# Macaron block on one core: attention scores in units of 32 queries for all heads, and half of the query blocks taken straight from the bank of the maxima

## The chip, the cores and the metric

The kernel runs on one core of one Trainium2 chip. The metric is device time in microseconds (us) of one launch, the median of a few runs.

## The reference

The input is x, 16 batches of 512 positions of 128 features, all in float32. Three residual steps follow each other: half a feed-forward step, an attention step, half a feed-forward step, each on the layer-normalised input.

```python
x = x + 0.5 * ffn(layernorm(x))      # ffn: x @ int4-rounded kernel + bias + (x @ a) @ b
x = x + attn(layernorm(x))           # 16 heads, causal
x = x + 0.5 * ffn(layernorm(x))
# attn: q = x Wq (16 heads of 64); latent = x Wkv_down (32 wide, shared by all heads)
#       k = latent Wk_up, v = latent Wv_up
#       y = softmax(mask(q k^T / 8)) v; result = y Wout
```

## The kernel before

**The algebra.** Query and key weights are multiplied once at the start, and so are value and output weights. Each head then has a 32-wide query against one 32-wide latent per key, and that latent is also the value. The 16 heads stand as 4 groups (`g`) of 4 heads (`h`); the four heads of a group lie on the four blocks of 32 partitions. `qt` holds the queries, `kt` the latents with features on partitions (the same four times), `lat` the latents with keys on partitions.

**Two passes over the scores.** The softmax needs the maximum of each query's scores, and the outputs need the probabilities with keys on partitions. So each score is computed twice. The S pass (`s_parts`, banks `sx`) puts queries on partitions and keys along the free axis; TensorE adds the causal mask of the last 128 by 128 block with small bfloat16 products (`mask_w`), and VectorE takes the negated maxima (`find_maxima`, L651 and L655). GpSimd splits the maxima into three bfloat16 terms (`maxima`, L728 to L732), and TensorE turns them into rows (`maxima_t`, tile `rows`). The T pass (`t_parts`, banks `tx`) puts keys on partitions and queries along the free axis; TensorE adds the turned maxima with bfloat16 products against `ones_u`, ScalarE takes the exponential (`exponentials`, L664, tile `pt`), and GpSimd zeroes the probabilities above the diagonal (`zeros`, L677).

**Outputs and sums.** `values` multiplies `lat` with `pt` for a group's four heads side by side, 128 by 32 products into the bank `o` (L763). The softmax's sums come from products with ones; GpSimd first adds blocks of `pt` so that fewer products are needed (`add_01`, `add_2`, `add_23`, lines L747, L752, L757). The sums go through DRAM to a compact form, VectorE takes reciprocals, DRAM broadcasts them (`rb`), and GpSimd multiplies (`normalise`, L839). `tail` projects with the merged value and output weights (`yp`), adds the residual, and does the second feed-forward step.

**The order.** It is written out by hand, under a manual schedule. A step is one `burst`: an S unit of 512 keys' worth of columns for four heads, and beside it a T unit of the same size of six steps earlier (`LAG`). `STEP` lists the five kinds of unit of a pair of groups; a batch has ten steps, 160 steps in all. `merge` interleaves the two streams so that heads 0 and 1 of T run beside heads 2 and 3 of S on the four row blocks of the array, and then the other way round. A burst has two S tiles of two banks each (pool `ps_s`, two buffers, 4 banks), and four T banks (pool `ps_t`, four buffers). Everything else is put between bursts: `plan` gives the pieces of `front` (layer norms, first feed-forward step, keys, queries), `latent`, `normalised` (the layer norms' inverse roots, with three VectorE operations in `ln_newton`, L344 to L346) and `tail` due times in steps. The last units, with no S work left, have bursts of their own (`late_burst`, `late_outputs`, `divided`, `last_tail`).

Of the kernel before, what the change touches and what calls it, by code (L numbers as in the profile page):

```python
# [25 lines left out]
def macaron_kernel(  # L26
# [24 lines left out]
    assert D == P and NT * P == L and L <= 512 and HG == 4 and H % HG == 0  # L51
    scale = HD**-0.5
# [4 lines left out]
    io = ctx.enter_context(tc.tile_pool(name="io", bufs=3))  # L57
# [54 lines left out]
    def load_heads(src, n, name):  # L112
        t = const.tile([P, NW, n], F32, tag=name, name=name)
        nc.sync.dma_start(t, src.rearrange("(t p) n -> p t n", p=P))
        return t

    wq_sb = load_heads(wq_t, D, "wq_sb")
    wk_sb = load_heads(wk_t, LD, "wk_sb")
    xs[1] = load_x(1)
    zs[1] = load_blocks(x[1], "a1")  # L120
    wv_sb = load_heads(wv_t, LD, "wv_sb")
    wo_sb = load_heads(wout, D, "wo_sb")
# [8 lines left out]
    terms = []  # L131
    for k in range(2):
        t3 = const.tile([P, NT, P], BF16, tag=f"terms{k}", name=f"terms{k}")
        nc.vector.memset(t3, 0.0)
        terms.append(t3)
    ones_u = const.tile([P, 2, P], BF16, tag="ones_u", name="ones_u")
# [6 lines left out]
    eye_b = const.tile([P, LD], BF16, tag="eye_b", name="eye_b")  # L143
    for h in range(HG):
        rows = slice(h * LD, (h + 1) * LD)
        nc.vector.tensor_copy(eye_b[rows, :], ident[rows, ts(h, LD)])
    eye2_b = const.tile([P, 2, LD], BF16, tag="eye2_b", name="eye2_b")
    for k in range(2):
        nc.vector.tensor_copy(eye2_b[:, k, :], eye_b)
    for u in range(2):  # L150
        pick = const.tile([P, 1], F32, tag=f"pick{u}", name=f"pick{u}")
        nc.vector.tensor_reduce(pick, ident.rearrange("p (h c) -> p c h", c=LD)[:, 3 * u : 3 * u + 3, :], AX.XY, ALU.max)
        nc.vector.tensor_scalar(ones_u[:, u, :], ones_f, pick, None, ALU.mult)


    mask_w = const.tile([P, NT, P], BF16, tag="mask_w", name="mask_w")
    nc.gpsimd.memset(mask_w, 0.0)

    def masks():
        for h in range(HG):  # L160
            rows = slice(h * LD, (h + 1) * LD)
            nc.gpsimd.affine_select(
                mask_w[rows, :, :], mask_w[rows, :, :], pattern=[[-LD, NT], [1, P]],
                compare_op=ALU.is_ge, fill=MASK, base=0, channel_multiplier=-1,
            )
# [87 lines left out]
    wqk_raw = act2.tile([P, L], F32, tag="osb", name="wqk_raw", bufs=4)[:, : NW * 2 * LD].rearrange(  # L253
# [97 lines left out]
    def ln_scale(src, name, ln):  # L351

        xn = act2.tile([P, NT, D], F32, tag="xn", name=f"xn_{name}")
        for t in range(NT):
            nc.scalar.activation(xn[:, t, :], src[:, t, :], AF.Copy, scale=rstd(ln, "b", t))  # L355
        return xn
# [7 lines left out]
    def turn_blocks(z, name, tag):  # L364
        xt = act2.tile([P, L], F32, tag=tag, name=f"{tag}_{name}")
# [3 lines left out]
    def turn(src, name, tag):  # L369
# [3 lines left out]
        xt = act2.tile([P, L], F32, tag=tag, name=f"{tag}_{name}")  # L373
# [3 lines left out]
    def with_bias(src, name, engine):  # L377
        xb = act2.tile([P, NT, D], F32, tag="xb", name=f"xb_{name}")
# [10 lines left out]
    def ffn(xt, ln, xb, name, tag, bufs):  # L389


        return ffn_out(ffn_product(xt, name), ln, xb, name, tag, bufs)

# [6 lines left out]
    def ffn_out(fp, ln, xb, name, tag, bufs):  # L400
        dst = io.tile([P, NT, D], F32, tag=tag, name=f"{tag}_{name}", bufs=bufs)
# [16 lines left out]
    def normalised(w):  # L418
        whats = [k for k, b in (("c", w - 2), ("b", w + 2), ("a", w + 3)) if 0 <= b < (B - 2 if k == "c" else B)]
# [7 lines left out]
    def front(b, st):  # L427
# [23 lines left out]
        x1 = st["x1"] = ffn(xt, la, xb, na, "x1", 5)  # L451
# [11 lines left out]
        xnt = turn_blocks(z, nb, "xnt_b") if b else turn(xn, nb, "xnt_b")  # L463
        yield
        mp = take(f"kt_ps_{b}")
        kt = st["kt"] = act2.tile([P, L], F32, tag="kt", name=f"kt_{b}", bufs=3)
# [21 lines left out]
        def query(g):  # L488
            mp = take(f"qt_ps_{b}_{g}")
            product(mp, wqk_flat[:, ts(g, P)], xnt)  # L490
            if g % 2 == 0:
                st["qt", g] = act2.tile([P, 2, L], F32, tag="qt", name=f"qt_{b}_{g}", bufs=4)
            nc.scalar.copy(st["qt", g - g % 2][:, g % 2, :], mp)  # L493

        yield
        query(0)
        yield
        query(1)
        yield
        query(2)  # L500
        yield
        query(3)
        yield

    def latent(b, st):

        lat = st["lat"] = act2.tile([P, NT, LD], F32, tag="lat", name=f"lat_{b}", bufs=3)
        for m in range(HG):
            keys = st["kt"][ts(m, LD), :].rearrange("c (t m r) -> c t m r", t=NT, m=HG)
            nc.vector.transpose(lat[ts(m, LD), :, :], keys[:, :, m, :])  # L510
        yield
# [3 lines left out]
    FRONT_STEPS = (-31, -30.5, -29, -28, -21, -19.25, -16, -16, -13, -10.5, -8, -4.25, -4, -3.5, -3.25, -2, 3, 4)  # L515
    SECOND_STEPS = (-9.5, -8.5, -7, -5.5, -5, -4.25, -4, -3.5, -3.25, -2, 3, 4)
    THIRD_STEPS = (-18.5, -18.5, -18.5, -18, -17.5, -17.25, -16, -16) + FRONT_STEPS[8:]
    FOURTH_STEPS = (-27, -26, -25.5, -25) + FRONT_STEPS[4:]
    TAIL_STEPS = (1.75, 2.5, 2.75, 3.5, 4.5, 7, 7, 7.75, 10.5)
    NORMALISED_STEPS = (5, 6)  # L520

    def tail(b, st, late=False):


# [38 lines left out]
        yield  # L563

# [544 lines left out]
```

## Time and profile before

| | |
|---|---|
| median of 3 runs | 810.46 us (810.18 to 812.5) |
| span of the profiled execution | 808.8 us, mean granted TensorE clock 0.995 |
| TensorE busy | 786.1 us, 97% |
| VectorE busy | 620.9 us, 77% |
| ScalarE busy | 488.1 us, 60% |
| GpSimd busy | 676.1 us, 84% |
| first S unit starts | 30.28 us into the span |
| first late burst starts | 767.76 us into the span |

The profile's span runs from the first to the last instruction of one execution; the median of the runs is 1.7 us longer. In the profile PE is TensorE's products, PEld its weight loads, DVE is VectorE, ACT is ScalarE, POOL is GpSimd and SP issues most transfers. A product in float32 stands as two instructions on TensorE, one for each of two passes. A line such as L651 is that of the instruction in the program; all products of a burst carry the line of `merge`, L641.

### The profile page before, as it was taken

How to read it: one execution, taken by the hardware profiler on the slowest of the kernel's cores; microseconds unless marked ns; L12 is line 12 of the kernel's file. 1: busy time of each engine (PE TensorE's matmuls, PEld its weight loads, DVE VectorE, ACT ScalarE, POOL GpSimd, SP SyncE). 2: the span in 40 equal slices, each digit the busy share in tenths (PEclk: the TensorE clock that was granted, in tenths of full speed). 3: DMA queues.
4: the chain of work that ended last, by engine and by line, in shares of the span. 5: the costliest groups of instructions: out<-in, count | busy, mean ns of one | idle time of the engine just before them, and what ended most of it. 6: DMA issues, size and time to landing. Idle time of an engine off the chain costs nothing.

```text
span 808.8 us, 35715 instructions
## 1 busy us (share of the span) xinstructions
PE 786.1 (97%) x15400; PEld 507.6 (63%) x15400; DVE 620.9 (77%) x1318; ACT 488.1 (60%) x971; POOL 676.1 (84%) x675
## 2 busy tenths in 40 slices
PE   7899999999999999999999999999999999999987
PEld 5556566675666667666666666666566666666644
DVE  7887886878878697877869787777978777686817
ACT  1237675657566675756657575666657666665661
POOL 1018989999988999989899898989989979998992
PEclk9989999999999999999999999999999999999999
DMA  5123122232422323332232423223223222211201
GB/s 138 28 57 68 32 69 68 65 72 73 95 61 70 80 62 83 74 83 60 70 89 55 93 63 82 69 61 93 51 53 77 58 63 66 70 44 47 58 24 48
DMA packets 171022, 54.01 MB, mean 67 GB/s; under 512 B 119512, under 2 KB 162680, under 8 KB 170864
## 3 DMA queue, kind: packets, MB, share of 16 engines
q1 hardware_dynamic: 170096, 51.44, 27.2%
q8 instruction: 120, 1.97, 1.0%
q10 hardware_dynamic: 768, 0.30, 0.1%
q14 instruction: 38, 0.31, 0.1%
HBM read 37.90 MB, written 13.80 MB: 64 GB/s over the span
## 4 chain that ended last, share of the span: by engine, by line
PE 70%; DVE 9%; POOL 6%; DMA 5%; ACT 5%; SPq 2%; issue 2%; DVEq 0%; POOLq 0%; ACTq 0%
PE sx L641 17%; PE o L763 14%; PE tx L641 13%; PE s L763 7%; PE qt_ps L385 6%; PE yp L385 6%; DVE nmax L651 3%; POOL b L747 3%; DMA rb<-recs 2%; PE fp_c L385 2%; ACT xn_b L355 2%; DMA recs<-rec 2%; PE fp_a L385 1%; POOL ot L839 1%; ACT pt L664 1%
## 5 line engine op out<-in xcount | busy, mean ns | idle before, releaser
L651 DVE TENSOR_REDUCE nmax<-sx 128x2 f32<-128x768 f32 (+2 forms) x384 | 312.6, 863 | 105.9 <-PE tx L641 67.6
L664 ACT ACTIVATE pt<-tx 128x512 f32<-128x512 f32 x616 | 319.5, 598 | 85.3 <-PE tx L641 78.8
L641 PE MATMUL sx<-kt,qt 32*128 32x512 f32 (+3 forms) x2048 | 324.4, 444 | 0.0
L641 PE MATMUL tx<-qt,kt 32*128 32x512 f32 x1728 | 319.3, 469 | 0.0
L747 POOL TENSOR_TENSOR b<-pt,pt 128x768 f32<-128x768 f32 x126 | 226.8, 1822 | 0.5
L641 PEld LDWEIGHTS sx<-kt,qt 32*128 32x128 f32 x2048 | 176.8, 186 | 24.7 <-issue 1.0
L677 POOL TENSOR_SCALAR_AFFINE_SELECT pt<-pt 128x1024 f32<-128x1024 f32 (+1 forms) x162 | 144.8, 900 | 17.2 <-ACT pt L664 15.4
L763 PE MATMUL o<-pt,lat 128*32 128x512 f32 x1984 | 146.4, 435 | 0.8 <-POOL pt L677 0.8
L641 PEld LDWEIGHTS tx<-qt,kt 32*128 32x128 f32 x1728 | 131.5, 185 | 5.1
L763 PEld LDWEIGHTS o<-pt,lat 128*32 128x32 f32 x1984 | 62.5, 109 | 77.9 <-issue 59.0
L641 PE MATMUL tx<-rows,ones_u 6*128 6x512 bf16 (+1 forms) x988 | 109.9, 297 | 1.1 <-DVE wvo L292 0.5
L839 POOL TENSOR_TENSOR ot<-osb,rb 128x512 f32<-128x512 f32 x62 | 79.0, 1275 | 35.9 <-DMA rb<-recs 33.6
L655 DVE TENSOR_REDUCE nmax<-sx 128x4 f32<-128x1024 f32 x64 | 75.4, 1219 | 31.9 <-PE tx L641 31.8
L782 ACT COPY osb<-o 128x512 f32<-128x512 f32 x62 | 36.3, 585 | 92.1 <-PE o L763 92.1
L641 PE MATMUL sx<-eye_b,mask_w 32*128 32x64 bf16 (+1 forms) x2560 | 87.8, 183 | 2.4 <-DVE nmax L655 1.7
L641 PEld LDWEIGHTS <-ones_u 6*128 6x128 bf16 x1024 | 43.1, 92 | 74.3 <-issue 61.6
L641 PEld LDWEIGHTS <-mask_w 32*128 32x128 bf16 x2560 | 67.4, 92 | 32.7 <-issue 24.6
L752 POOL TENSOR_TENSOR b<-b,pt 128x512 f32<-128x512 f32 x63 | 80.5, 1278 | 5.1
L757 POOL TENSOR_TENSOR b<-pt,pt 128x512 f32<-128x512 f32 x63 | 80.4, 1276 | 0.1
L385 PE MATMUL qt_ps<-xnt_b_b,wqk 128*32 128x512 f32 x512 | 68.0, 603 | 0.2
L763 PE MATMUL s<-b,ones_f 128*32 128x384 f32 x992 | 65.1, 380 | 3.1 <-POOL b L752 2.6
L493 ACT COPY qt<-qt_ps 128x512 f32<-128x512 f32 x64 | 37.5, 586 | 48.4 <-PE qt_ps L385 48.4
(194 smaller groups left out, 815.6 us busy)
## 6 DMA issues: line engine op xcount, KB each, us to landing
rb<-recs SPq DMA_DIRECT2D x248, 64.0 KB
x<-in_x_dram SPq DMA_DIRECT2D x16, 256.0 KB
sums<-ssb SPq DMA_DIRECT2D x248, 2.0 KB
z_a<-in_x_dram SPq DMA_DIRECT2D x60, 64.0 KB
blocks_b<-xn_b SPq DMA_DIRECT2D x15, 256.0 KB
z_b<-blocks_b SPq DMA_DIRECT2D x60, 64.0 KB
kt<-kt_d SPq DMA_DIRECT2D x60, 64.0 KB
out_dram<-x_c SPq DMA_DIRECT2D x15, 256.0 KB
```

Source lines behind the costliest of these rows:

```text
L385: nc.tensor.matmul(dst[ts(h, LD), :], lhsT=w[:, ts(h, LD)], rhs=mv, start=start, stop=stop, skip_group_check=True)
L493: nc.scalar.copy(st["qt", g - g % 2][:, g % 2, :], mp)
L641: nc.tensor.matmul(dst, lhsT=w, rhs=mv, start=first, stop=last, skip_group_check=True)
L651: nc.vector.tensor_reduce(nmax[:, i, heads, u], sx[:, :, col : col + (i + 1) * P], AX.X, ALU.max, negate=True)
L655: nc.vector.tensor_reduce(nmax[:, 1, heads, :], sx.rearrange("p k (u n) -> p k u n", u=2), AX.X, ALU.max, negate=True)
L664: nc.scalar.activation(pt[:, :, 2 * pair + k, :], tx[k].rearrange("p (b n) -> p b n", n=P), AF.Exp)
L677: nc.gpsimd.affine_select(diag, diag, pattern=[[0, diag.shape[1]], [1, P]], compare_op=ALU.is_ge, fill=0.0, base=0, channel_multiplier=-1,)
L747: nc.gpsimd.tensor_tensor(*flat, ALU.add)
L752: nc.gpsimd.tensor_tensor(b01, b01, st["pt", 2, g][:, u], ALU.add)
L757: nc.gpsimd.tensor_tensor(both, st["pt", 2, g][:, 2 + u], st["pt", 1, g + u][:, 0], ALU.add)
L763: nc.tensor.matmul(dst[ts(h, LD), :].rearrange("p (b n) -> p b n", n=P), lhsT=w[h] if isinstance(w, list) else w, rhs=mv, start=start, sto ...
L839: nc.gpsimd.tensor_tensor(turned(st)[:, g, :], st["osb", g], st["rb", g], ALU.mult)
```

## The change

A unit is no longer four heads of one group and 128 queries; it is all 16 heads and 32 queries. The queries are stored as query-major, group-minor (`qt` as 512 times 4), so that 128 columns are 32 queries by 4 groups, and the four row blocks carry the four `r` of a group. Each of the 16 query blocks of a batch has its own key width, a multiple of 32. Nine S units cover a batch (`S_UNITS`), seven T units cover its second 256 queries (`T_UNITS`).

- **Query blocks 0 to 7** (the first 256 queries, "short") have no T pass. ScalarE takes the exponential straight from the S bank with the maximum as bias, and keeps the sum along the row (`short_exponentials`). VectorE turns the result in 32 by 32 blocks in the next step (`turn_short`). Outputs are 128 products per batch of 32 by 32 weights (`short_values`), once all of a batch is turned. The sums need no products (`short_reciprocals`).
- **Query blocks 8 to 15** go as before, except that the causal mask of the T pass is now in the bfloat16 products (`diag_w`), so GpSimd's `zeros` is gone. GpSimd adds whole `pt` tiles (128 by 2048) five times a batch (`add`), and `sums` streams two added tiles instead of summing per group.
- S masks are four small products per unit (`tri`, `eye4`) instead of sixteen.
- The order is again written out by hand, nine steps a batch, 144 in all. The special ending is gone: the loop runs on until all planned work is done.

```diff
+    S_UNITS = ((12, 2), (13, 1), (14, 0), (15,), (7,), (8, 6), (9, 5), (10, 4), (11, 3))
+    T_UNITS = {5: (3, 0), 6: (3, 1), 7: (3, 2), 8: (3, 3), 10: (2, 0), 11: (2, 1), 12: (2, 2)}
+    SHORT = 2 * NT
...
     def find_maxima(...):
+        for qb, (w, col) in zip(unit, widths(unit)):
+            nc.vector.tensor_reduce(
+                st["nmax"][:, slot(qb), ts(pair, 2)], sx[:, :, col : col + w], AX.X, ALU.max, negate=True
+            )
+    def exponentials(tx, st, unit, pair):
...
+        for k in range(2):
+            nc.scalar.activation(pt[:, 2 * pair + k, :], tx[k], AF.Exp)
+    def short_exponentials(sx, st, unit, pair):
...
+        for qb, w, col in mine:
+            pq = probs.tile([P, 2, L // 2], F32, tag="pq", name=..., bufs=4)
+            for k in range(2):
+                r = 2 * pair + k
+                nc.scalar.activation(
+                    pq[:, k, :w], sx[:, k, col : col + w], AF.Exp, bias=st["nmax"][:, slot(qb), r : r + 1],
+                    accum_out=st["total"][:, qb // NT, r, qb % NT : qb % NT + 1],
+                )
+            turning.append((st, qb, pair, pq[:, :, :w]))
+    def turn_short():
+        while turning:
+            st, qb, pair, pq = turning.popleft()
+            nc.vector.transpose(
+                st["short"][:, ts(pair, 2), : qb + 1, qb, :], pq.rearrange("p k (n c) -> p k n c", c=LD)
+            )
     def burst(n, s_at, t_at, t_unit):
...
+        for k in range(2):
+            if s_at:
+                find_maxima(ss[k], s_at, s_unit, 1 - k)
+            if t_at:
+                exponentials(tt[k], t_at, t_unit, k)
+        for k in range(2):
+            if s_at:
+                short_exponentials(ss[k], s_at, s_unit, 1 - k)
-    def zeros(st, g, kind, u, heads=slice(0, 4)):
...
+    def add(st, name, one, two):
...
+        nc.gpsimd.tensor_tensor(st[name], st[one], st[two], ALU.add)
+    def values(st, i):
+        o_ps = take(f"o_{st['b']}_{i}")
+        for j in range(i + 1):
+            streamed(o_ps, st["lat"][:, j, :], st["pt", i, j], j == 0)
+        st["osb", i] = act2.tile([P, L], F32, tag="osb", name=..., bufs=3)
+        nc.scalar.copy(st["osb", i], o_ps)
+    def short_values(st):
+        banks = [take(f"o_{st['b']}_s{p}") for p in range(HG)]
+        for kb in range(SHORT):
+            for p in range(HG):
+                rows = ts(p, LD)
+                for r in range(HG):
+                    nc.tensor.matmul(
+                        banks[p][ts(r, LD), kb * LD : SHORT * LD], lhsT=st["lat32"][rows, kb, :],
+                        rhs=st["short"][rows, r, kb, kb:, :].rearrange("p n c -> p (n c)"), ...
+                    )
...
+        for p in range(HG):
+            nc.scalar.copy(...)          # 4 copies of 128 by 256, out of the four banks
+    def short_reciprocals(st):
+        nc.vector.reciprocal(rec, st["total"]...)   # 128 by 32
+        nc.vector.transpose(rec_t, rec)
...
+    GAPS = {
+        0: ((short_values, (), 1), (maxima_t, (2,), 1)),
+        4: ((values, (2,), 1), (maxima_t, (3,), 0)),
+        5: ((sums, (3,), 1),),
+        6: ((sums, (2,), 1),),
+        8: ((values, (3,), 0),),
+    }
+    NORMALISED = {5: ((0, 1), (1, 1)), 0: ((3, 2),), 1: ((2, 2),)}
+    ADDED = {
+        7: (("a3", ("pt", 3, 0), ("pt", 3, 1), 0),),
+        0: (("a3b", ("pt", 3, 2), ("pt", 3, 3), 1),),
+        1: (("a3", "a3", "a3b", 1),),
+        3: (("a2", ("pt", 2, 0), ("pt", 2, 1), 1),),
+        4: (("a2", "a2", ("pt", 2, 2), 1),),
+    }
+    TERMS = {3: slice(0, 4), 8: slice(4, 8)}
...
+    while n < END or todo:
+        turn_short()
+        parts(n - 0.5)
+        for name, one, two, lag in ADDED.get(s, ()): ...   # add
+        burst(n, batch(n, 0), *t_due(n))
...                                                        # maxima, normalise
+        parts(n - 0.25)
+        for what, which, lag in GAPS.get(s, ()): ...
+        parts(n)                                           # NORMALISED_STEPS = (5, 6): ln_newton at step 6
...
-    late_burst((st, gp), 4)
...
-    last_tail(st, yp, late_tail)
```

## The prediction

> **What bounds the kernel now.** I read the page first, then the windows of three batches in mid-run, then the groups kept apart by shape, then the timeline around single bursts and around the layer norm's small operations.
>
> ```profile
> PE 786.1 (97%) x15400; PEld 507.6 (63%) x15400; DVE 620.9 (77%) x1318; ACT 488.1 (60%) x971; POOL 676.1 (84%) x675
> ```
>
> ```profile
> 438.60:485.60 47.00, 46.76 (x956) 30.36 (x952) 37.36 (x77) 30.11 (x61) 42.51 (x43) 1.00 0.32 74
> 485.60:532.60 47.00, 46.85 (x956) 30.37 (x952) 36.75 (x79) 30.20 (x61) 43.03 (x43) 1.00 0.31 73
> ```
>
> The columns of a window are its length, then busy time of PE, PEld, DVE, ACT and POOL. A batch takes 47.0 us, and TensorE is busy in 46.8 of them: it sets the time, at a granted clock of 1.00. VectorE has 10 us to spare, ScalarE 17, GpSimd 4. So work taken from TensorE counts fully until another engine, or a loop of waits, takes over.
>
> The prices come from these groups (columns at the end: busy us, mean ns of one):
>
> ```profile
> L664 ACT ACTIVATE pt<-tx 128x512 f32<-128x512 f32 x616 | 319.5, 598 | 85.3 <-PE tx L641 78.8 <-PE sx L641 2.7 <-POOL xb_a L379 1.6
> ...
> L747 POOL TENSOR_TENSOR b<-pt,pt 128x768 f32<-128x768 f32 x126 | 226.8, 1822 | 0.5
> ...
> L651 DVE TENSOR_REDUCE nmax<-sx 128x2 f32<-128x1024 f32 x128 | 152.7, 1219 | 43.7 <-PE tx L641 42.1 <-PE sx L641 1.0
> ...
> L752 POOL TENSOR_TENSOR b<-b,pt 128x512 f32<-128x512 f32 x63 | 80.5, 1278 | 5.1
> ...
> L651 DVE TENSOR_REDUCE nmax<-sx 128x2 f32<-128x256 f32 x128 | 53.1, 415 | 0.0
> ...
> L510 DVE STREAM_TRANSPOSE lat<-kt 32x128 f32<-32x128 f32 x64 | 19.2, 300 | 0.8
> ...
> L355 ACT ACTIVATE xn_b<-x_a,r_w 128x128 f32<-128x128 f32 x56 | 17.9, 392 | 0.0
> ...
> L366 DVE STREAM_TRANSPOSE xt_a_a<-z_a 128x512 f32<-128x512 f32 x15 | 10.7, 711 | 0.4
> ```
>
> **TensorE, per batch.** Out of the 47.0: four `values` of 2.3 us, four `sums` of 1.1, queries 3.8, projection 3.9, feed-forward and small things 2.9; the ten bursts have the other 22.8. After: seven bursts with T, at 2.2 (one in the timeline lasts from 488.39 to 490.58), and two with S alone, 1.1 and 0.6: 17.1. `values`: seven key blocks, each two passes 0.454 apart in the trace: 6.4. `sums`: 1.8. Queries, projection and the rest stay, 10.6. New are the 32 by 32 products. Each of the 16 array tiles streams 1152 columns twice; at 0.454 us for 512 columns that is 2.0 us if all sixteen run at once, and 8.2 if only four do. Records of different tiles start 6 to 13 ns apart (eight mask products take 0.25 us, one takes 0.17), so 256 records need 1.7 to 3.3 us to start. I take 3.3, the issue bound, as it is nearest to the mask rows. The sum is 39.2 us.
>
> [...]
>
> **VectorE, per batch.** Maxima: 17408 elements in place of 20480, 32 instructions in place of 28. The rows give 1.04 ns an element and 0.15 us fixed (0.1 back to back): 24.2 falls to 21.1. Turning: 16 transposes of 64 to 512 elements; by L510 and L366 0.163 us plus 1.07 ns an element, 7.5 us in all. One 256-wide transpose for `lat32` adds 0.4. So 36.9 becomes 41.7, if nothing else changes. The write pattern of the turning is in chunks of 32, which no row shows; I give it no charge.
>
> **ScalarE, per batch.** 28 exponentials of 512 in place of 40, at 0.52: 20.8 to 14.6. New are 32 short ones, 32 to 256 wide, mean 144, with a per-partition bias and a row sum. The nearest row is `xn_b`, 128 wide with a per-partition scale, 0.32 each back to back (17.9 us over 56); 0.84 ns an element beyond it. The sum's cost is not shown: between nothing and another fixed part, 0.21; I take 0.1, so 0.43 each, 13.8 us. Copies: two `osb` and two `ssb` fewer, four of 256 more, -0.9. Total 30.1 to 36.8.
>
> [...]
>
> **GpSimd, per batch.** `zeros` goes (9 us). From 1822 ns at 768 and 1278 at 512, an add costs 2.13 ns an element: one of 2048 takes 4.5 us, five 22.7. With `normalise` (5.1), terms and biases: 33 in place of 42.9. Plenty of room, but in long pieces.
>
> **No engine is then above 42 us, so the waits decide.** The S banks are now held longer. Before, VectorE released them after the maxima; now ScalarE does, and its short exponentials stand behind the four exponentials of T in its queue, and behind the maxima. Next step's burst waits for that, and all of TensorE's queue behind it; VectorE's turning waits for ScalarE too, with the next maxima queued behind. From the release of the first S tile to the next such release: 1.3 us until the first exponential of T can start (488.39 to 489.73 in the timeline below), 2.1 for four, 0.95 for two short ones: 4.4. Those steps that have both (5 to 8) can't be shorter, though TensorE's own work in them is 3 to 4.
>
> ```profile
> 488.39 0.39 PE L641 MATMUL tx<-rows,ones_u 6*128 6x512 bf16 x2
> ...
> 489.73 2.08 ACT L664 ACTIVATE pt<-tx 128x512 f32<-128x512 f32 x4 [0.62 <-PE tx L641]
> ...
> 490.33 0.25 PE L641 MATMUL sx<-eye_b,mask_w 32*128 32x32 bf16 x8
> ```
>
> Laid out step by step, in us: step 0 (S alone, a short wait for the last turning, 3.3 of small products, four copies of 0.28 before T's banks are free) 5.4; step 1 (burst, two feed-forward products) 4.4; step 2 5.1, as VectorE comes late from step 1 with 6.4 of its own; step 3 (burst, two queries) 4.3; step 4 (maxima, values 2.7, turned maxima, two queries) 6.5; steps 5, 6 and 7 by the loop, 4.4, 4.9 (two operations of the layer norm, 0.5, on ScalarE) and 4.4; step 8 (burst 2.2, values 3.65) 5.9. Sum 45.3, against 47.0.
>
> **The layer norm against the long adds.** This takes the gain back:
>
> ```profile
> 473.43 3.59 POOL L747 TENSOR_TENSOR b<-pt,pt 128x768 f32<-128x768 f32 x2
> ...
> 474.12 1.16 DVE L344 SCALAR_TENSOR_TENSOR e_w<-mv_w,y_w 128x12 f32<-128x12 f32 x1
> ...
> 475.31 1.73 DVE L345 SCALAR_TENSOR_TENSOR e_w<-e_w,y_w 128x12 f32<-128x12 f32 x1
> 477.08 0.17 DVE L346 SCALAR_TENSOR_TENSOR r_w<-e_w,y_w 128x12 f32<-128x12 f32 x1
> ```
>
> A 12-element operation with two SBUF inputs takes 0.16 us when GpSimd is quiet, but here 1.16 and 1.73: it ends when GpSimd's running add ends (adds of 1.8 us from 473.43 and 475.21). In the change these three operations stand at the end of step 6, behind its maxima, and GpSimd's next add (a3, 4.5 us) starts when the last exponential of step 6 ends. By my layout the exponentials end some 0.6 us ahead of the maxima. The layer norm then waits about 4 us, with step 6's turning and step 7's maxima queued behind it, and TensorE waits for the S banks. Of the 4 us, step 8's slack takes 0.8: +3.2 a batch, 48.5.
>
> **The sum.** First S unit at 30.28 before, +3.1 for three more queries: 33.4. The first batch, half empty, 38 (before, its six steps without T took 22). Fifteen batches of 45.3: 679.5. The collision in fourteen: 44.8. The end has no special order any more: the last three T units, adds of 4.5, sums through DRAM, projection, feed-forward, one behind the other: 50, against 41 before. Lighter first and last batches: -4. That is 841.7 of span, +1.7 as before between span and median: 843 us, against 808.8 and 810.46.
>
> **Rivals.** (a) Faster: the layer norm gets in ahead of the add. Place: end of step 6; price: the 44.8; it decides if step 6's maxima end before its fourth exponential does, 0.6 us from my layout. Then 799 us. For it: exponentials a little slower than I priced them push the add back. Against: VectorE is the fullest engine just there. Chance 0.27. (b) The banks do not bind and TensorE alone sets the time, about 41 a batch: 734 us. Against it speaks the order of ScalarE's queue. Chance 0.04. (c) The small products run four at a time, 8.2 us instead of 3.3, all of it exposed in step 0: +78, so 921, or 877 without the collision. Chance 0.10. (d) The row sums cost 0.21 each: +0.2 on each step's loop, +25: 868. Chance 0.09. The forecast itself, 820 to 860, has 0.50. The built order has 448 exponentials of T, 512 short ones and 256 turnings, so the change does what it says.
>
> **Range and chances.** From 785, where (a) meets cheap row sums, to 890, which takes in (d) and (c) without the collision; beyond lie (b) and the worse half of (c). Faster by over 0.3% (about what a measurement of this kernel can tell): most of (a), (b) and the lower edge of the forecast, 0.30; same 0.03; slower 0.67.
>
> **What would show it.** Right: TensorE idle before S products behind ScalarE's `pq`, at some 80% busy; one operation of the layer norm at about 4 us, and a batch of 48 us. Wrong: layer norm operations at 0.2 us; short products far from 3.3 us a batch; turning above 7.5 us; a batch below 43.

## The result: slower by 14.7%, and the profile after

The changed kernel takes 931.58 us (median of 4 runs, 923.07 to 936.65), against 811.05 us of the kernel before on the same chips (810.18 to 812.5). The ratio is 1.1468, 95% interval 1.1409 to 1.1527. The forecast was 843 us with a range of 785 to 890: the side was right, the size was not. The profiled execution took 923.07 us, with a span of 921.1. All sums of parts below are made on that span; it is the shortest of the four (the other three took 931 to 937), so the parts add up to some 8 us less than the median has. Of the experiments, one execution (the profiled one of Newton's step early, 1142.78 us) ran at a clock of 0.55 throughout and is left out of the comparisons.

The page's busy times, and its row of the granted clock in 40 slices:

```profile
PE 765.4 (83%) x14096; PEld 451.1 (49%) x14096; DVE 711.3 (77%) x1650; ACT 597.5 (65%) x1811; POOL 577.5 (63%) x353
...
PEclk9859999989999899989998998999799999999785
```

TensorE is busy for only 21 us less than before, and is now idle for 17% of the span instead of 3%. And its clock, 0.995 before, falls below full speed again and again.

The windows (length, then busy time of PE, PEld, DVE, ACT, POOL, then the clock) cut the span at the first and at the last batch's 32 by 32 products (`o_s` in the profile); a batch of mid-run is between:

```profile
0.00:92.00 92.00, 68.91 (x616) 42.64 (x616) 68.79 (x207) 39.59 (x119) 21.99 (x33) 0.81 0.27 58
...
447.70:498.30 50.60, 43.75 (x876) 25.86 (x872) 42.81 (x98) 36.92 (x112) 35.72 (x22) 0.97 0.29 69
...
92.00:855.30 763.30, 664.83 (x12832) 389.34 (x12828) 627.51 (x1400) 546.55 (x1667) 522.91 (x310) 0.95 0.26 61
855.30:921.10 65.80, 31.68 (x656) 19.11 (x652) 15.01 (x43) 11.32 (x25) 32.58 (x12) 0.71 0.21 50
```

So the forecast's sum, part by part: start and first batch 92.0 us where 71.4 were forecast (33.4 and 38); fifteen batches 763.3, or 50.9 each, where 724.3 were (679.5 and 44.8); the end 65.8 where 46 were (50 and -4). The excess is 20.6, 39.0 and 19.8 us.

The forecast's collision is there. The timeline at the end of step 6 and into step 8 of one batch (start, duration; in brackets the idle time before, and what ended it):

```profile
481.69 4.53 POOL L741 TENSOR_TENSOR a<-pt,pt 128x2048 f32<-128x2048 f32 x1 [2.27 <-ACT pt L661]
481.82 4.43 DVE L369 SCALAR_TENSOR_TENSOR e_w<-mv_w,y_w 128x12 f32<-128x12 f32 x1
...
486.58 1.03 DVE L688 STREAM_TRANSPOSE short<-pq 128x384 f32<-128x384 f32 x2
487.54 2.45 DVE L651 TENSOR_REDUCE nmax<-sx 128x2 f32<-128x704 f32 x4
...
489.73 0.20 PE L639 MATMUL sx<-tri,eye 32*128 32x64 bf16 x2 [2.72 <-ACT pq L678]
```

GpSimd's sum starts 0.13 us ahead of the layer norm's first operation, which then takes 4.43 us instead of 0.16 and ends with the sum. Turning and maxima are late by as much, and TensorE stands idle for 2.72 us before step 8. What the forecast did not have comes next: the clock's record shows half speed from 489.85 us, for 3.41 us.

Not every such hole brings it. The run has fifteen holes of 2.7 us in front of step 8, and half speed follows ten of them. All stretches of half speed begin on one grid, whole multiples of 3.413 us from the first at 39.29. The ten holes lie with at least 1.88 us inside one interval of this grid; the other five lie across a boundary, with at most 1.68 us on either side.

The second surprise is inside the small products:

```profile
447.73 3.57 PE L765 MATMUL o_s<-short,lat 32*32 32x256 f32 x235
453.11 0.32 PE L765 MATMUL o_s<-short,lat 32*32 32x32 f32 x21 [1.81 <-issue]
```

235 of 256 records run at 15 ns each, with 292 ns the mean length of one, so they do overlap as forecast. Then TensorE stops for 1.81 us and waits for nothing that the profile shows ("issue"). Stops of 0.65 to 1.8 us stand in 12 of the 16 batches, 13 in all; half speed begins within 2.8 us of the end of seven of them, not of the one above.

The other terms of the change, from the groups (busy us, mean ns, idle before):

```profile
L678 ACT ACTIVATE pq<-sx,nmax 128x160 f32<-128x160 f32 (+7 forms) x512 | 189.4, 389 | 127.8 <-DVE nmax L651 123.5 <-PE wvo_ps L312 4.2
...
L678 ACT ACTIVATION_READ_ACCUMULATOR pq<-sx,nmax 128x1 f32 x512 | 109.8, 214 | 0.0
...
L369 DVE SCALAR_TENSOR_TENSOR e_w<-mv_w,y_w 128x12 f32<-128x12 f32 (+2 forms) x18 | 72.1, 4005 | 6.9 <-ACT y_w L364 6.9
...
L516 ACT COPY qt<-qt_ps 128x512 f32<-128x512 f32 x64 | 65.3, 1134 | 2.2 <-PE qt_ps L410 2.2
```

The row sum shows as a record of its own, 214 ns, but it overlaps its exponential: two of them start 0.34 to 0.42 us apart at 128 to 224 wide, less than the 0.43 priced for the mean. The query copies, which the forecast let stay, take 1134 ns instead of 586, as they now write every fourth element.

### The profile page after: what moved, and what is told of

Its sections match the earlier page's. It is cut to its first block, busy times and chain, and to the rows that moved or that the text cites. A ratio compares the mean times of both kernels' runs of the same rounds, so it can differ in the third digit from the quotient of the medians.

```text
span 921.1 us, 34036 instructions
## 1 busy us (share of the span) xinstructions
PE 765.4 (83%) x14096; PEld 451.1 (49%) x14096; DVE 711.3 (77%) x1650; ACT 597.5 (65%) x1811; POOL 577.5 (63%) x353
## 4 chain that ended last, share of the span: by engine, by line
PE 40%; DVE 39%; ACT 8%; issue 6%; DMA 5%; POOL 1%; SPq 1%; DVEq 0%; ACTq 0%; POOLq 0%
DVE nmax L651 17%; PE o L746 10%; PE sx L639 9%; DVE e_w L369 8%; PE tx L639 7%; PE o_s L765 7%; ACT pq L678 5%; DVE short L688 3%; DMA blocks_c<-x 2%; PE qt_ps L410 2%; DVE x L422 2%; DMA z_c<-blocks_c 2%; DVE xb_c L422 2%; DVE st_w L351 1%; PE fp_a L410 1%
## 5 line engine op out<-in xcount | busy, mean ns | idle before, releaser
L651 DVE TENSOR_REDUCE nmax<-sx 128x2 f32<-128x832 f32 (+15 forms) x512 | 338.9, 711 | 93.5 <-PE sx L639 70.6
L639 PE MATMUL sx<-kt,qt 32*128 32x416 f32 (+15 forms) x2048 | 312.5, 458 | 2.7 <-ACT qt L516 1.8
L661 ACT ACTIVATE pt<-tx 128x512 f32<-128x512 f32 x448 | 238.2, 595 | 82.6 <-PE tx L639 65.5
L639 PE MATMUL tx<-qt,kt 32*128 32x512 f32 x896 | 284.0, 703 | 2.1 <-ACT rows L735 2.1
L678 ACT ACTIVATE pq<-sx,nmax 128x160 f32<-128x160 f32 (+7 forms) x512 | 189.4, 389 | 127.8 <-DVE nmax L651 123.5
L741 POOL TENSOR_TENSOR a<-pt,pt 128x2048 f32<-128x2048 f32 x32 | 145.2, 4539 | 117.7 <-ACT pt L661 117.7
L639 PEld LDWEIGHTS sx<-kt,qt 32*128 32x128 f32 x2048 | 179.9, 206 | 65.8 <-issue 47.1
L688 DVE STREAM_TRANSPOSE short<-pq 128x192 f32<-128x192 f32 (+7 forms) x256 | 110.6, 455 | 47.1 <-ACT pq L678 24.2
L639 PE MATMUL sx<-tri,eye 32*128 32x64 bf16 (+1 forms) x576 | 56.1, 194 | 76.7 <-ACT pq L678 68.7
L678 ACT ACTIVATION_READ_ACCUMULATOR pq<-sx,nmax 128x1 f32 x512 | 109.8, 214 | 0.0
L639 PEld LDWEIGHTS tx<-qt,kt 32*128 32x128 f32 x896 | 87.2, 208 | 16.8 <-ACT rows L735 11.7
L639 PEld LDWEIGHTS <-eye 32*128 32x128 bf16 x576 | 36.1, 103 | 119.1 <-issue 105.6
L639 PE MATMUL tx<-rows,ones_b 3*128 3x512 bf16 x320 | 77.3, 416 | 9.2 <-DVE xb_c L422 8.1
L369 DVE SCALAR_TENSOR_TENSOR e_w<-mv_w,y_w 128x12 f32<-128x12 f32 (+2 forms) x18 | 72.1, 4005 | 6.9 <-ACT y_w L364 6.9
L741 POOL TENSOR_TENSOR a<-a,pt 128x2048 f32<-128x2048 f32 x16 | 73.3, 4580 | 2.4 <-DMA out_dram<-xb_c 2.4
L741 POOL TENSOR_TENSOR a3b<-pt,pt 128x2048 f32<-128x2048 f32 x16 | 72.6, 4536 | 0.0
```

The costliest lines, as they stand in the source:

```text
L369: nc.vector.scalar_tensor_tensor(e, var, EPS, y, ALU.add, ALU.mult)
L639: nc.tensor.matmul(dst, lhsT=w, rhs=mv, start=first, stop=last, skip_group_check=True)
L651: nc.vector.tensor_reduce(st["nmax"][:, slot(qb), ts(pair, 2)], sx[:, :, col : col + w], AX.X, ALU.max, negate=True)
L661: nc.scalar.activation(pt[:, 2 * pair + k, :], tx[k], AF.Exp)
L678: nc.scalar.activation(pq[:, k, :w], sx[:, k, col : col + w], AF.Exp, bias=st["nmax"][:, slot(qb), r : r + 1], accum_out=st["total"][:, qb ...
L688: nc.vector.transpose(st["short"][:, ts(pair, 2), : qb + 1, qb, :], pq.rearrange("p k (n c) -> p k n c", c=LD))
```

## The experiments

Theory A: the wait of L369 for GpSimd, with the half clock that its hole brings on, is most of what a batch takes over 45.3 us. Rival B: the way of an S bank through ScalarE (maxima, T exponentials, short exponentials, next products) sets the batch, and the wait lies beside it. "Batch" below is the mean over 15 batches, from the first o_s product of the first to that of the last, in the profiled execution.

### The wait: moved, shortened, its hole filled

**Newton's step early** (the inverse roots' three operations, the first at L369).

```diff
-    NORMALISED_STEPS = (5, 6)
+    NORMALISED_STEPS = (4.75, 5.5)
```

> Newton's three VectorE instructions (L369 to L371) are put ahead of the maxima of step 6 instead of behind step 6, so that they run before GpSimd's first 4.5-us sum a3 begins; nothing else changes. Theory A (the wait of L369 for GpSimd's sum, about 4 us of VectorE in each batch, and the stretches of half clock that the hole it leaves in TensorE brings on, are most of what the batches take over 45.3 us): L369 falls from 4.0 us to under 0.5 us each, TensorE's holes of 2.7 us in step 7 go, the batch falls from 50.9 us to 45 to 47 us, and the time from 931 to 855 to 875 us. Rival B (the loop in which an S bank goes from the products through maxima and exponentials back to the products would set the batch anyway, and the wait lies beside it): L369 falls in the same way, and the time stays above 910 us.

Measured: 870.43 us (the middle one of three executions, 867.66 to 872.42), ratio 1.0713 (1.0677 to 1.0750). The profile of the direct end further down, which has this edit too, serves for the wait and the batch: L369 takes 155 ns in the mean, and fifteen batches take 716.6 us, so one takes 47.8 instead of 50.9 (45 to 47 were expected):

```profile
L369 DVE SCALAR_TENSOR_TENSOR e_w<-mv_w,y_w 128x12 f32<-128x12 f32 (+2 forms) x18 | 2.8, 155 | 0.6 <-ACT y_w L364 0.6
...
89.00:805.60 716.60, 651.25 (x12832) 381.12 (x12828) 570.67 (x1400) 544.97 (x1667) 518.06 (x308) 0.96 0.29 65
```

The gain is 61 us: Theory A's figure, against B's.

**The sums in four pieces.**

```diff
-        nc.gpsimd.tensor_tensor(st[name], st[one], st[two], ALU.add)
+        for r in range(HG):
+            nc.gpsimd.tensor_tensor(st[name][:, r, :], st[one][:, r, :], st[two][:, r, :], ALU.add)
```

> Each of GpSimd's sums of 128 x 2048 is issued as four sums of 128 x 512; Newton's step stays where it was. If L369 waits for the GpSimd instruction that is running, and for that one alone, it falls from 4.0 us to 1.3 us or less (a quarter of 4.5 us at most, and its own 0.2 us), and the time by Theory A lies between 860 and 890 us. If the wait is for the data of the whole sum or for something else that does not depend on the length of GpSimd's instruction, L369 stays near 4 us and the time near 931 us. By rival B L369 falls and the time stays above 910 us.

Measured: 885.72 us, ratio 1.0901 (1.0875 to 1.0928). The groups of the first two operations:

```profile
L370 DVE SCALAR_TENSOR_TENSOR e_w<-e_w,y_w 128x12 f32<-128x12 f32 (+2 forms) x18 | 21.2, 1180 | 0.6
L369 DVE SCALAR_TENSOR_TENSOR e_w<-mv_w,y_w 128x12 f32<-128x12 f32 (+2 forms) x18 | 15.8, 876 | 6.8 <-ACT y_w L364 6.8
```

Each operation now waits for one quarter of a sum (1.27 us in the mean), and L370 is caught as well, which had run free before at 0.17 us in the median. With GpSimd's instructions at 1.27 us in place of 4.54, L369 fell from 4.0 to 0.88 us in the mean; the whole sum was not shorter, four quarters of 1.27 us, so it was not the whole sum that L369 waited for.

**The hole filled, first in the wrong place.** Seven products of the identity ahead of the products of step 7, into a T bank that the true products overwrite.

```diff
+        if t_at and s_at and n % STEPS == 7:
+            for _ in range(7):
+                nc.tensor.matmul(tt[0][0][:, :P], lhsT=ident, rhs=ident, start=True, stop=True)
```

> The wait of L369 stays; ahead of the products of step 7 TensorE gets seven products of the identity with itself into a T bank that the true products overwrite, some 2.6 us of work for the hole of 2.7 us. By Theory A with the clock as a part of its own: the stretches of half clock behind step 7 go (3.4 us each, 12 or so of them), which gives back 1 to 1.7 us each, 15 to 25 us in all (931 to about 905 to 915 us); the wait itself stays. If the clock costs nothing, because other waits hide it, the time stays within 5 us of 931 us; if the products fill time that was not idle, it rises by up to 40 us.

Measured: 936.05 us, ratio 1.1533 (1.1466 to 1.1599). A miss: VectorE runs behind, so a wait at the end of step 6 makes its hole at the start of step 8. The products ran one step too early (1.83 us a batch), and the hole remained at 2.27.

**The hole filled in the right place.**

```diff
+        if t_at and s_at and n % STEPS == 8:
+            for _ in range(11):
+                nc.tensor.matmul(tt[0][0][:, :P], lhsT=ident, rhs=ident, start=True, stop=True)
```

> As the filled step before, but the products of the identity stand where the hole is, ahead of the products of step 8 (the unit with the diagonal masks), eleven of them, some 2.8 us; the wait of L369 stays at 4.4 us. If the clock is a part of its own in what the wait cost: the stretches of half clock that begin 2 us behind the hole go, and the time falls by 12 to 30 us (to 900 to 920 us). If the half clock costs nothing because VectorE holds these steps anyway, the time stays within 5 us of 931 us.

Measured: 909.58 us, ratio 1.1204 (1.1173 to 1.1234), 22 us less than the change. L369 is as long as ever:

```profile
L369 DVE SCALAR_TENSOR_TENSOR e_w<-mv_w,y_w 128x12 f32<-128x12 f32 (+2 forms) x18 | 72.1, 4007 | 6.4 <-ACT y_w L364 6.4
```

The mean granted clock of the profiled execution is 0.937, against 0.916 in the change's. Between the first and the last o_s products the clock's record has 37.5 us of half speed where the change has 81.9; 44.4 us at half speed are worth 22.2 us of work. The wait's 61 us are thus some 22 of clock and 39 of the wait itself. That split goes by the medians; between the two profiled executions the spans differ by 16 us (921.1 and 905.1), so the clock's part is known to within some 6 us.

### Rival B: the order on ScalarE

**Short exponentials of the first tile ahead of the second T tile's.**

```diff
                 exponentials(tt[k], t_at, t_unit, k)
-        for k in range(2):
             if s_at:
                 short_exponentials(ss[k], s_at, s_unit, 1 - k)
```

> In each step ScalarE takes the short exponentials of the first S tile ahead of the T exponentials of the second T tile, instead of after all T exponentials. Rival B (the loop of the S bank through ScalarE sets the steps that have T exponentials): the first S bank comes free 1.2 us earlier in steps 5 to 8 of each batch, up to 4.8 us a batch, and the time falls by 30 us or more (to under 900 us). Theory A: the steps behind the wait are held by VectorE, not by the order on ScalarE, the T banks come free later by as much as the S banks come earlier, and the time stays within 12 us of 931 us.

Measured: 875.37 us, ratio 1.0786 (1.0730 to 1.0842). By the time alone, B had won. The group says otherwise:

```profile
L369 DVE SCALAR_TENSOR_TENSOR e_w<-mv_w,y_w 128x12 f32<-128x12 f32 (+2 forms) x18 | 8.3, 464 | 6.2 <-ACT y_w L364 6.2
```

The last T exponential now comes later, GpSimd's sum starts behind Newton's step, and the wait is gone (median 161 ns). The edit had removed A's wait by accident, so both edits were put together:

> Both edits in one: Newton's step ahead of the maxima of step 6, and the short exponentials of the first S tile ahead of the second T tile's. Either alone took L369's wait away (the second because GpSimd's sum then starts later) and gave back 56 to 60 us. If that wait was all that either edit removed, the two together give no more than one: 865 to 878 us. If the order on ScalarE has a worth of its own (the loop of the S bank, rival B), the two together give another 15 us or more: below 856 us.

Measured: 882.15 us, ratio 1.0881 (1.0825 to 1.0937). That is 12 us above Newton's step alone, and above both expectations: the order adds nothing, and its own worth is nil or less.

**Without the row sums** (with Newton's step early).

```diff
+            nc.gpsimd.memset(st["total"], 1.0)
...
-                    accum_out=st["total"][:, qb // NT, r, qb % NT : qb % NT + 1],
```

> On top of Newton's early step (871 us): the short exponentials write no row sums (the sums' tile is filled with ones, so the outputs of the first eight query blocks are not normalised); the reading records of 0.21 us behind each of them go. If the row sums lie on the path (rival of the forecast, 0.21 us each, or 0.1 by the distance between two exponentials): 32 a batch, half of them in steps that ScalarE holds, 1.6 to 3.4 us a batch, and 818 to 847 us. If ScalarE's length doesn't set the steps once the wait of L369 is gone: within 10 us of 871 us.

Measured: 853.52 us, ratio 1.0515 (1.0492 to 1.0537). The kernel leaves the first eight query blocks unnormalised. The gain is 17 us, or 0.033 us for each of 512, between the two expectations: some of ScalarE's length counts, much less than its records add up to (109.8 us).

**Queries in a row** (with Newton's step early).

```diff
-            nc.scalar.copy(qt.rearrange("p (q g) -> p g q", g=NG)[:, g, :], mp)
+            nc.scalar.copy(qt[:, ts(g, L)], mp)
```

> On top of Newton's early step (871 us): ScalarE writes the queries of a batch in a row instead of every fourth element, so the copies should take 0.59 us as in the kernel before, not 1.13 (the queries then stand in another order, so the outputs differ; instructions and sizes are the same). If these copies are on the path: four a batch, 2.2 us in all, 30 to 35 us of the whole, and 836 to 845 us. If they lie beside other work: within 10 us of 871 us.

Measured: 865.99 us, ratio 1.0657 (1.0614 to 1.0701), not told apart from Newton's step alone. The products are as many and as large, but the queries stand in another order. The copies are back at 588 ns; 28 us of ScalarE's work lay beside other work.

### The stop in the small products

**Half of the products left out** (the wait is kept).

```diff
-        for kb in range(SHORT):
+        for kb in range(0, SHORT, 2):
```

> Leaves out every second block of keys in the 32 by 32 products (64 products of 128 in each batch); all else stays, so the time alone is read. If TensorE's instruction stream is what stops it for 1.2 to 1.9 us in each batch near the end of these products, the stop goes with half of them, the groups fall from 5.1 us to 2.0 to 2.5 us, and the time falls by 20 to 50 us (the stop, half of the products, and the stretch of half clock that follows). If the products lie beside other waits, the groups fall and the time stays within 10 us of 931 us.

Measured: 885.22 us, ratio 1.0935 (1.0880 to 1.0991). The 64 products take 2.12 us in nearly every batch, with no stop; 46 us less. That is 2.9 a batch for a group that is 3.0 shorter, so hardly anything covers these products in step 0. The run takes away half of the products and the stop together; it does not tell the two apart.

What goes with the stop, the change's trace shows. Queue q8, "instruction", carries 110 transfers of 16384 bytes, and TensorE has 28192 records, some 256 for each transfer. In each of the 13 stops over 0.6 us, one of these transfers started 0.5 to 1.8 us before the stop, and the stop ended 2.2 to 2.7 us after that start (450.66 and 453.11 in the batch above). The place is the same too: with TensorE's products, weight loads and semaphore records counted in order of their start (28402), the last product before the stop is the 193rd of a row of 256, in all 13. With two records for the weights and two for the passes, 128 products are 512 records, twice 256, in some 4 us of running time, where the run's mean is one transfer in 8.4 us. So the stop keeps step with these transfers; that TensorE waits there for instructions that come too late is the author's reading, and no run shows it by itself.

**Two rounds of 64**, two banks in step 0 and two in step 1 (Newton's step early; `short_values` takes the banks it is to fill).

```diff
-        0: ((short_values, (), 1), (maxima_t, (2,), 1)),
+        0: ((short_values, ((0, 1),), 1), (maxima_t, (2,), 1)),
+        1: ((short_values, ((2, 3),), 1),),
```

> On top of Newton's early step (871 us): the 128 small products of a batch are done in two rounds of 64, two row blocks (two banks) in step 0 and two in step 1. With half of the products left out, 64 took 2.12 us and had no stop. If the stop is one of instructions that come too slowly for a long row of short ones: two groups of 2.1 to 2.6 us, no stop of over 1 us inside them, and 840 to 862 us. If TensorE needs all four row blocks at once to do sixteen at a time: each group takes 4 us or more, TensorE's work grows by 3 us a batch, and the time is 900 us or more.

Measured: 903.48 us, ratio 1.1133 (1.1113 to 1.1152). The stop is gone (rounds of 2.35 and 2.50 us). The two together take 4.9 us where one row without a stop takes 3.9 to 4.5, so two row blocks are a little slower than four, far from twice. But the time rises by 33 us, outside both expectations, and the timeline tells why:

```profile
497.33 2.50 PE L765 MATMUL o_s<-short,lat 32*32 32x256 f32 x128
...
499.98 0.64 DVE L688 STREAM_TRANSPOSE short<-pq 128x192 f32<-128x192 f32 x2 [4.93 <-PE o_s L765]
500.54 2.45 DVE L651 TENSOR_REDUCE nmax<-sx 128x2 f32<-128x896 f32 x4
```

`short` has one buffer; the next batch's first turning waits for the second round, with the maxima behind it.

**Two rounds, and the unit of query block 15 in front**, so that this turning comes a step later.

```diff
-    S_UNITS = ((12, 2), (13, 1), (14, 0), (15,), (7,), ...
+    S_UNITS = ((15,), (12, 2), (13, 1), (14, 0), (7,), ...
```

> On top of Newton's early step (871 us): two rounds of 64 small products in steps 0 and 1, as before (there 903 us, with a new hole of 2.8 us in TensorE because VectorE's first turning of the next batch waits for the second round and the maxima stand behind it), and the S unit of the last query block alone (15) is moved to the front of the batch, so that the next batch's first turning comes a step later. If the stop of 1.2 to 2 us in the row of 128 and the half clock behind it are what holds the batches above 45.3 us: no stop, no new hole, a batch of 45.3 to 46.3 us, and 838 to 856 us. If something else holds them: the stop goes, and the time stays above 862 us.

Measured: 851.27 us, ratio 1.0482 (1.0440 to 1.0525), the shortest version that does the whole computation. A batch takes 46.5 us, and the clock stays full, as window and clock row show:

```profile
387.00:434.00 47.00, 43.38 (x882) 26.40 (x879) 39.18 (x99) 36.93 (x114) 36.06 (x22) 1.00 0.33 73
```

```profile
PEclk9856999999999999999999999999999999999875
```

**The same with the wait**, Newton's step behind step 6 again.

> The two rounds of small products with the last query block's unit in front, and Newton's step where the change has it (behind step 6). Against 851 us with Newton's step early. If wait and half clock cost what the earlier runs gave (38 us for the wait with its hole filled, 22 more for the clock): 889 us where TensorE's clock stays full behind the hole, 911 us where it halves. If the other order of units moves GpSimd's sum away from Newton's step, L369 falls to under 1 us and the time stays near 851 us.

Measured: 916.86 us, ratio 1.1280 (1.1217 to 1.1343); batch 50.7. The wait is back:

```profile
L369 DVE SCALAR_TENSOR_TENSOR e_w<-mv_w,y_w 128x12 f32<-128x12 f32 (+2 forms) x18 | 72.1, 4008 | 6.3 <-ACT y_w L364 6.3
```

By the medians the wait costs 66 us without the stop and 61 with it; the stop (with what the other order of units may do) costs 15 with the wait and 19 without. So they are two causes, and by the medians they add up. The profiled executions show the stop's part in the batches only where the wait is gone (47.8 and 46.5 us); with the wait the batch is 50.9 with the stop and 50.7 without, so the 15 is the less certain figure. Half clock follows either cause, and does not add up: between first and last o_s products it is 82 us in the change, 61 with the stop alone (the direct end's profile, clock 0.96 there) and 7 without both (clock 1.00); with the wait alone the profiled execution's mean clock is 0.915, against 0.916 in the change's.

**The same without the wait, short exponentials first**, B's last chance.

> Newton's early step, the two rounds, the other order of units (851 us together), and the short exponentials of the first S tile ahead of the second T tile's. If the S bank's way through ScalarE still holds the steps with T units: 825 to 842 us. If TensorE, busy 43.4 of 46.5 us in a batch there, is now the bound: 846 to 860 us.

Measured: 874.70 us, ratio 1.0764 (1.0719 to 1.0809), outside both expectations: the order is now worse by 23 us. It lets the first tile out earlier and the second later, and a wait of the products for the second stands in the timeline, in step 4:

```profile
353.89 0.19 PE L639 MATMUL sx<-tri,eye 32*128 32x32 bf16 x2 [1.32 <-ACT pq L678]
```

Whether such waits are the 23 us is not shown. Over the whole run TensorE waits less for `pq` than in the run before (34.2 us for 44.9); what has doubled is ScalarE's wait for the maxima (83.5 us for 41.8).

### Start and end

**Both kept busy**: twelve products of the identity behind each of the first five steps and of those behind the last S unit.

```diff
-        if not parts(n) and n < LAG:
-            keep_clock(4)
+        parts(n)
+        if n < LAG or n >= END:
+            keep_clock(12)
```

> Twelve products of the identity (1.6 us at full clock) behind every one of the first five steps and of the steps after the last S unit, where there were four behind some of the first; the batches between are as they were. If half clock is what made the first batch 21 us and the end 17 us longer than forecast: the stretch of half clock from 39 to 70 us goes, the first o_s products come at 80 us instead of 92, and the time falls by 10 to 25 us. If the first batch is a loop of waits (maxima, exponentials, next products) and the end a chain of transfers and single instructions: the first o_s products come at 87 us or later, and the time stays within 8 us of 931 us.

Measured: 964.91 us, ratio 1.1874 (1.1832 to 1.1917). From 25 to 66 us the clock was now full (the mean of the profiled execution is 0.936, against 0.916 in the change's), and the first o_s products still came at 92.9 us. That does not quite clear the clock: twelve idle products took 2.9 us, not the 1.6 expected, and two groups of them stand in the chain of the first batch:

```profile
55.11 2.87 PE idle L196 x24
...
58.98 2.88 PE idle L196 x24
```

So the first batch is not 21 us too long for want of clock, but up to 5 us of it may be. Of the 36 us by which the span rises, 29 are at the end, where the idle products stood ahead of the last true ones.

**S products tile by tile** in steps without T (with Newton's step early).

```diff
         elif s_at:
-            merge(*s_seq)
+            for seq in s_seq:
+                merge(seq)
```

> On top of Newton's early step (871 us): in the steps without a T unit (five in the first batch, two in each later one) the products of the second S tile follow those of the first, instead of taking turns with them; so the first tile's products no longer wait for the second tile's bank. If the way of the S banks (products, maxima of two tiles, two exponentials, next products) holds these steps: 1 us or more of each, the first o_s products come at 82 to 85 us instead of 89, and the time falls to 840 to 862 us. If VectorE or the half-width use of TensorE (two row blocks at a time) sets them: the first o_s products come at 88 us or later and the time is 868 to 900 us.

Measured: 868.91 us, ratio 1.0685 (1.0632 to 1.0738); first o_s products at 90.3 us (89.0 in the direct end's profile). No effect. Together with the two rounds:

> Newton's early step, the two rounds with the other order of units, and the products tile by tile, all together. If the gains of the last two add: 812 to 840 us, near the kernel before. If both give back the same idle time, or neither gives any: 850 to 880 us.

Measured: 851.30 us, ratio 1.0489 (1.0450 to 1.0527): the two rounds' gain, and nothing else.

**The last batch's sums straight from the exponentials**, without GpSimd (with Newton's step early); `sums` and `reciprocals` of the last batch are called in the steps END, END + 1, END + 4 and END + 5.

```diff
-        for n_, part in enumerate(SUMMED[i]):
+        for n_, part in enumerate(SUMMED[i] if b < B - 1 else [("pt", i, j) for j in range(i + 1)]):
...
-            if batch(n, lag):
+            if batch(n, lag) and batch(n, lag)["b"] < B - 1:
                 add(batch(n, lag), name, one, two)
```

> On top of Newton's early step (871 us): the last batch has no sums on GpSimd; TensorE sums its exponentials straight from the five to seven tiles in the steps after the last S unit, and the reciprocals follow one step later. By the end's chain (GpSimd's sums, 4.5 us each, up to 851 us, then sums, reciprocals and broadcasts one behind the other): the time from the last o_s products to the end falls from 58 to 66 us to 48 to 54 us, and the whole to 858 to 866 us. If transfers and not GpSimd hold the end: within 5 us of 871 us.

Measured: 870.92 us, ratio 1.0747 (1.0714 to 1.0779), nothing gained:

```profile
805.60:868.40 62.80, 35.49 (x696) 19.82 (x692) 10.02 (x43) 11.33 (x25) 15.05 (x8) 0.72 0.23 53
```

GpSimd has half the work of the change's end (15.05 us for 32.58), and the stretch is 62.8 us long all the same, near the 63.9 of the run with queries in a row. In the chain of that end TensorE's pieces stand in turn with transfers: sums, reciprocals and broadcasts through DRAM one after the other.

## Why the prediction was wrong, by its own steps

The excess over the forecast's span is 79 us: 39 in the fifteen batches, 20.6 up to the first batch's small products, 19.8 at the end. The steps that failed are two costs in the batches that were put at nothing, half clock behind idle holes (some 22 us) and the stop in the small products (15 to 19), TensorE's bursts, which were priced too short, and the first batch and the end, which were both priced too short.

**The collision** was right in place, order and cause, and nearly right in size: 44.8 us priced, 39 measured with its hole filled.

**The clock** is the term that was missing. The forecast read a granted clock of 1.00 before and took it over to a kernel for which it had itself forecast TensorE idle in every batch. The wait's share was some 22 us. Half speed came behind ten of the fifteen holes of 2.7 us, those with 1.88 us or more inside one interval of the record's grid of 3.413 us, and also near the end of stops of 1.03 to 1.57 us in the small products. What makes the clock fall was not shown beyond that.

**The small products.** Priced 3.3 us a batch, issue-bound. The issue bound was right in kind (15 ns a record, 3.9 us a batch), and rival (c) was wrong: half of the row blocks cost 2.35 to 2.5 us for half of the products. What was missed is the stop, 15 to 19 us of the whole with its half clock. That 931 us lies near (c)'s 921 is chance.

**The loop of 45.3 us** without a collision: measured 46.5 with wait and stop gone, at full clock. The excess there is 1.2 a batch, 18 us in all, and TensorE is busy for 43.4 of each 47 us where the forecast had 39.2. The larger part of that is the bursts (L639): 20.8 us busy in such a batch where 17.1 were priced, from the length of a single burst. The two rounds of small products have 4.9 where 3.3 were. So it was TensorE rather than the order on ScalarE that was nearly the bound, as far as its busy share tells; no run shortened the bursts. That the loop's length came out close does not make its mechanism right: of B's experiments only the row sums gave anything.

**Row sums**: priced 0.1 us each, measured 0.033 on the path; rival (d), 0.21, falls. The 0.84 ns an element in the price of the short exponentials is the step from L664 to L668 in the kernel before, 598 ns at 512 wide and 1029 at 1024. **Query copies**: "stay" was false by 28 us of ScalarE, which cost nothing that could be told apart.

**The first batch**, 38 us priced, took 58.6. "Half empty" was the mistake: half empty of work, but each step's chain is whole. The order of tiles is ruled out, and by the run with the idle products the clock is worth some 5 us at most. The chain of waits has one more wait of 4.13 us at L369; without it the first o_s products come 3 us earlier (89.0 in the direct end's profile). It also has VectorE's one-time work (masks, four copies of `wvo`, statistics) standing ahead of maxima; how much that is worth was not separated, and most of the 20.6 us stays open.

**The end**, 46 us priced, took 65.8, of which GpSimd's sums are no part. Part of it is the clock again: it is 0.71 over this stretch, against 0.99 in the last 41 us of the kernel before. The same 64 products of the projection, in the chain of the end and in mid-run:

```profile
873.36 3.67 PE yp L410 x64
...
484.91 1.95 PE L410 MATMUL yp<-wvo,ot 128*32 128x128 f32 x64
```

TensorE's pieces of that chain which ran at half speed come to 17.7 us, so an estimate of what the clock costs there is half of that, some 9 of the 19.8 us. For the rest the chain points at the round trips through DRAM, one behind the other; no run shortened those or gave the clock back without adding work, so both stay argued.

Rival (a) shows how much hung on the missing terms: without the collision it had 799 us, and that kernel takes 870.

## What to carry to other kernels

When a change leaves TensorE idle in holes, price each hole with the clock it may lose afterwards, not by its length alone: here ten of fifteen holes of 2.7 us were followed by 3.41 us at half speed each. Where the hole can't go, idle products in just that place can give clock back (half speed in the batches fell from 81.9 to 37.5 us); where true products wait behind them they cost time (2.9 us for twelve in the chain of the first batch). A 12-element VectorE operation took 4.4 us here while a GpSimd sum of 4.5 us ran, and 0.16 when none did; maxima and turnings under the same sums took as long as elsewhere (1.02 us at 832 wide, 0.68 at 512). So look for such a small operation beside long GpSimd instructions, and put it ahead of them or cut them. And when an edit gives the expected gain, look at the suspected wait before crediting the theory: the edit may have removed another's cause.

## What had not been expected of the hardware

- Half clock came after ten of fifteen holes of 2.7 us, those with 1.88 us or more inside one interval of a fixed grid of 3.413 us, in stretches of 3.41 us, and elsewhere in stretches of 3.41 or 6.83; 82 us of them between the first and the last o_s products, where the kernel before had 7.8 in its whole span.
- In rows of 512 short TensorE records a stop came in 12 of the change's 16 batches, always behind the 193rd of 256 in the count of all TensorE records, until 2.2 to 2.7 us after a 16 KB instruction transfer had begun; rows of 256 ran through in nearly every batch (0.6 us of idle time in all of them with half of the products, 0.9 in the two rounds).
- The wait went with the length of GpSimd's instruction: 4.43 us behind one of 4.53, 0.88 to 1.18 us in the mean behind quarters of 1.27.
- A ScalarE copy that writes every fourth element of float32 took 1134 ns where one in a row took 588.
